# A pad of 384 bytes per partition at the top of SBUF's right side, in a sparse-linear and LoRA-gate kernel

## The chip, the core and the metric

One core of a Trainium2 chip. The metric is the device time of one execution in microseconds (us). Times come from runs on the chip, details from one execution taken by the hardware profiler.

## What is computed

Input is `x`, 2 batches of 1024 rows of 1024 fp32 values. With `xn` the layer norm of each row:

```python
bm  = 32x32 blocks of mask whose sum is > 0
s   = xn @ (W * bm).T + bias                      # 1024 -> 1024
c   = softmax((mean over rows of xn) @ Wq.T @ keys.T / sqrt(128))   # 8 coefficients per batch
g   = silu(xn @ W_org.T + sum_e c[e] * (xn @ down[e]) @ up[e])      # 8 experts of rank 64
out = x + s * g
```

The kernel folds the experts into one matrix for each batch, `Y = W_org.T + down @ (c * up)`, so that each batch needs two products of 1024 x 1024 x 1024: one with the masked `W` ("s") and one with `Y` ("y").

## The kernel before

Every fp32 operand of a large product is split into a high and a low part of type float32r, and each product is three matmuls: high x high, high x low, low x high. Nearly all matmuls have a stationary operand of 128 x 128 and a moving operand of 128 x 512.

**Order of the work.** Batch 0 comes first. A ramp of about 60 us, ordered by hand, normalises rows, masks `W` and runs "s" for the left half of the columns. `phase` (L533), and `s_tile` (L1068) for the last half, then run eight row tiles per half; one row tile is `open_gemm` (L440), 24 matmuls at each of L450, L453 and L454 (stationary `xgrp`, moving `slot`). Between the row tiles stands the folding of `Y`: `y_mul` (L409), 12 matmuls at L414 to L416 (stationary `dhi` or `dlo`, moving `cut`, output `psw`), for batch 0 and then for batch 1. `late_stores` write batch 1's `Y` to DRAM (`yu`, issued at L510), from where it is read back.

Batch 1, from 291.92 us, is done otherwise: `quad` (L1223) computes a unit of the output from seven products of half matrices instead of eight. One product (`product`, L1209) is 12 matmuls, all of L1213: stationary `ow`, moving `xw`. There are eight units (L1074), alternately the first and the second factor of an output piece; each has 84 matmuls, into the PSUM tiles `acc_ps` and `py`. Written out, the order of one unit on TensorE is: product into `acc_ps`, one into `py`, three into `acc_ps`, one into `py`, one into `acc_ps` (unit 0 interleaves its first two; the last unit does its last product in two halves of 256 columns). While a unit runs, ScalarE and VectorE make `ow` for the next one: mask (L1091), sums (L1099), high part (L1105, ScalarE), low part (L1106, VectorE). ScalarE also copies partial sums between PSUM tiles in `quad` (L1243, L1273, and L1220 to SBUF); TensorE's next products wait for these copies. [...]

**Where tiles lie.** A pool is allocated from the left or from the right end of SBUF. L1103 takes `ow[u]` from `opools[u % 2]`: pool `o0` (L1152) is on the right, `o1` (L1300) on the left. So the even units' stationary operand lies on the right, the odd units' on the left, and the moving operand `xw` (L1053) lies on the left for all units. The byte addresses within a partition that the built program has are:

| tiles | side | address | modulo 512 |
|---|---|---|---|
| `slot`, `xgrp`, later `xw` (four) | left | 5728, 38496, 71264, 104032 | 96 |
| `raw`, then `ow` of odd units, `gate` | left | 136800, 151136, from 179808 | 96 |
| `misc`, and `stash`, `mine` | left | 152160, and from 162432 | 96, and 128 |
| `stage`: `ds`, `wo`, `us`, `ws`, `xt`, later `xs`, `rest`, `yt` | right | from 188384 | 480 |
| `dhi`, `dlo`, later `ow` of even units | right | 200672 to 206816, 200672 | 480 |
| `cu`: `cut`, `acc`, `xlate`, `mh`, `ml` | right | 208864 to 229343 | 480 |

PSUM is not touched by the sides.

Of the kernel before, what the change touches and what calls it, by code (L numbers as in the profile page):

```python
# [9 lines left out]
F32 = mybir.dt.float32  # L10
# [7 lines left out]
P = 128  # L18
# [14 lines left out]
def kernel(  # L33
# [28 lines left out]
    def open_pool(name, bufs=1, **kw):  # L62
        cm = tc.tile_pool(name=name, bufs=bufs, reuse_waits="tile", **kw)
        return cm, cm.__enter__()
# [13 lines left out]
    c0pool = for_late("const0", 1)  # L78
    stash_p = for_late("stash", 8)
    stage_l = for_late("stage_l", 2)  # L80
    fold_cms = []
    for_fold = lambda name, bufs: (fold_cms.insert(0, open_pool(name, bufs, side="right")), fold_cms[0][1])[1]
    cupool = for_fold("cu", 5)
# [1283 lines left out]
```

## Time and profile before

| | |
|---|---|
| time, median of 3 runs (lowest, highest) | 451.43 us (451.36, 451.67) |
| the profiled execution's own time | 452.2 us |
| its span, first to last instruction | 450.5 us |
| TensorE clock granted | 0.999 of full |
| weight loads (PEld) busy | 363.7 us, 81% |
| VectorE (DVE), ScalarE (ACT), GpSimd (POOL) busy | 288.9, 175.7, 76.4 us |
| moved by DMA | 90.58 MB, 201 GB/s over the span |

A row of the profile names the line, the engine, the operation and the tiles (out<-in), then the count, the busy time and the mean duration. Two things matter for reading it here. Matmuls are pipelined: the duration of one, from its start to its modelled end, reaches over the start of the next, so that the pace of a row of matmuls is not its mean duration but the distance from one start to the next. And the chain of waits (the work that ended last, followed back from the end) merges neighbouring matmuls of one line and tile to a piece of so many; a piece's length divided by its count is that pace.

### The profile page before, as it was taken

The numbers are of one execution on the slowest core, as the hardware profiler recorded it, in microseconds if no ns is written. First come the engines' busy times: TensorE is split into PE (matmuls) and PEld (weight loads), VectorE is DVE, ScalarE is ACT, GpSimd is POOL, SyncE is SP. The second block draws the span as 40 slices with busy tenths as digits, with TensorE's granted clock in tenths as the row PEclk, the third lists the DMA queues.
The fourth block names the chain that finished last, engine by engine and source line by source line (L and its number), as shares of the span: only waits on it lengthen the run. The fifth ranks groups of instructions, "written<-read, shape, count | busy, mean of one in ns | idle before, by whom it ended". The sixth has DMA issues, their size and how long they took to land.

```text
span 450.5 us, 5791 instructions
## 1 busy us (share of the span) xinstructions
PE 440.4 (98%) x2058; PEld 363.7 (81%) x2058; DVE 288.9 (64%) x478; ACT 175.7 (39%) x291; POOL 76.4 (17%) x93
## 2 busy tenths in 40 slices
PE   8999999999999999999999999999999999999996
PEld 6789888888878888878887788887888888888885
DVE  6989777766627778864466667487456294365625
ACT  4676535454731222233233135067344322441520
POOL 3774210002220313120000000110020030002000
PEclk9999999999999999999999999999999999999999
DMA  8995306677896889896978987865183146218103
GB/s 280 391 353 198 134 25 210 235 240 224 252 291 184 262 259 331 275 346 192 283 211 284 317 244 226 244 178 187 39 187 140 47 112 170 93 23 218 42 1 116
DMA packets 47741, 90.58 MB, mean 201 GB/s; under 512 B 4816, under 2 KB 15328, under 8 KB 47712
## 3 DMA queue, kind: packets, MB, share of 16 engines
q1 hardware_dynamic: 30624, 66.08, 43.7%
q0 software_dynamic: 6624, 16.26, 15.5%
q10 hardware_dynamic: 10464, 7.87, 5.3%
q8 instruction: 16, 0.26, 0.2%
q14 instruction: 13, 0.11, 0.1%
HBM read 70.26 MB, written 19.93 MB: 200 GB/s over the span
## 4 chain that ended last, share of the span: by engine, by line
PE 68%; DVE 11%; DMA 11%; issue 6%; ACT 3%; POOL 1%; SPq 0%; ACTq 0%; DVEq 0%; POOLq 0%
PE acc_ps L1213 25%; PE py L1213 10%; PE acc_ps L454 7%; PE acc_ps L450 7%; PE acc_ps L453 7%; PE psw L416 4%; PE psw L414 4%; PE psw L415 4%; DMA ws<-in_wT_dram 3%; DMA stash<-in_x_dram 2%; DMA yu<-wo 2%; DVE st L145 1%; DVE slot L591 1%; DMA raw<-in_x_dram 1%; DMA raw<-in_mask_dram 1%
## 5 line engine op out<-in xcount | busy, mean ns | idle before, releaser
L1213 PE MATMUL acc_ps<-xw,ow 128*128 128x512 f32 (+1 forms) x492 | 113.3, 387 | 0.0
L1213 PEld LDWEIGHTS acc_ps<-xw,ow 128*128 128x128 f32 x492 | 91.0, 188 | 19.8 <-ACT acc_ps L1273 0.4
L450 PE MATMUL acc_ps<-slot,xgrp 128*128 128x512 f32 (+1 forms) x288 | 106.5, 370 | 0.1
L454 PE MATMUL acc_ps<-slot,xgrp 128*128 128x512 f32 (+1 forms) x288 | 105.7, 367 | 0.7 <-DVE xgrp L603 0.7
L453 PE MATMUL acc_ps<-slot,xgrp 128*128 128x512 f32 (+1 forms) x288 | 105.7, 367 | 0.6 <-DVE slot L591 0.4
L453 PEld LDWEIGHTS acc_ps<-slot,xgrp 128*128 128x128 f32 x288 | 54.4, 189 | 10.7 <-DVE slot L591 2.1
L454 PEld LDWEIGHTS acc_ps<-slot,xgrp 128*128 128x128 f32 x288 | 54.2, 188 | 10.2 <-DVE xgrp L603 1.1
L450 PEld LDWEIGHTS acc_ps<-slot,xgrp 128*128 128x128 f32 x288 | 54.3, 188 | 9.1 <-DVE stash L466 0.3
L416 PE MATMUL psw<-cut,dlo 128*128 128x512 f32 x128 | 50.0, 390 | 1.2 <-DVE dlo L406 1.2
L414 PE MATMUL psw<-cut,dhi 128*128 128x512 f32 x128 | 50.0, 390 | 0.0
L415 PE MATMUL psw<-cut,dhi 128*128 128x512 f32 x128 | 49.8, 389 | 0.0
L1213 PE MATMUL py<-xw,ow 128*128 128x512 f32 x192 | 46.8, 392 | 0.0
L1213 PEld LDWEIGHTS py<-xw,ow 128*128 128x128 f32 x192 | 36.1, 188 | 7.9
L1106 DVE TENSOR_TENSOR ow<-raw,ow 128x1024 fp32r<-128x1024 f32 (+1 forms) x32 | 34.5, 1088 | 10.9 <-ACT ow L1105 10.9
L405 ACT CAST dhi<-ds 128x512 fp32r<-128x512 f32 x32 | 19.7, 617 | 39.3 <-DMA ds<-in_down_dram 17.0
L502 POOL DMA_DIRECT2D stash<-in_x_dram x16 | 14.4, 898 | 121.5 <-DVE stash L499 121.5
L421 DVE TENSOR_TENSOR wo<-wo,psw 128x512 f32<-128x512 f32 x32 | 21.9, 685 | 16.3 <-PE psw L416 16.0
L1105 ACT CAST ow<-raw 128x1024 fp32r<-128x1024 f32 (+1 forms) x32 | 29.4, 941 | 2.2 <-DVE wo L421 1.6
L416 PEld LDWEIGHTS psw<-cut,dlo 128*128 128x128 f32 x128 | 24.0, 188 | 6.6 <-DVE dlo L406 1.6
L414 PEld LDWEIGHTS psw<-cut,dhi 128*128 128x128 f32 x128 | 24.0, 188 | 5.3 <-ACT dhi L405 0.4
L415 PEld LDWEIGHTS psw<-cut,dhi 128*128 128x128 f32 x128 | 24.1, 188 | 5.0
L1196 POOL DMA_DIRECT2D gate<-in_xT_dram x12 | 10.5, 909 | 94.2 <-DVE gate L1190 68.8
(180 smaller groups left out, 480.5 us busy)
## 6 DMA issues: line engine op xcount, KB each, us to landing
ds<-in_down_dram SPq DMA_DIRECT2D x32, 256.0 KB, 3.6
wo<-in_worgT_dram SPq DMA_DIRECT2D x32, 256.0 KB, 3.8
raw<-in_x_dram SPq DMA_DIRECT2D x11, 512.0 KB, 4.8
stash<-in_x_dram POOLq DMA_DIRECT2D x16, 256.0 KB, 5.2
raw<-in_wu_dram SPq DMA_DIRECT2D x8, 512.0 KB, 4.9
yu<-wo ACTq DMA_DIRECT2D x16, 256.0 KB, 4.9
raw<-yu SPq DMA_DIRECT2D x8, 512.0 KB, 3.6
out_dram<-stash ACTq DMA_DIRECT2D x14, 256.0 KB, 3.9
```

The costliest lines, as they stand in the source:

```text
L405: nc.scalar.copy(dhi, ds)
L414: nc.tensor.matmul(ps, lhsT=dhi[:, c, :], rhs=u[c][:, 0, :], start=c == 0, stop=False)
L415: nc.tensor.matmul(ps, lhsT=dhi[:, c, :], rhs=u[c][:, 1, :], start=False, stop=False)
L416: nc.tensor.matmul(ps, lhsT=dlo[:, c, :], rhs=u[c][:, 0, :], start=False, stop=c == 3)
L421: nc.vector.tensor_tensor(ws, ws, ps, ALU.add)
L450: nc.tensor.matmul(ps, lhsT=xs[:, kt, 0, cols], rhs=w[:, kt, 0, wc], start=kt == 0, stop=False)
L453: nc.tensor.matmul(ps, lhsT=xs[:, kt, 0, cols], rhs=w[:, kt, 1, wc], start=False, stop=False)
L454: nc.tensor.matmul(ps, lhsT=xs[:, kt, 1, cols], rhs=w[:, kt, 0, wc], start=False, stop=kt == NKT - 1)
L502: nc.gpsimd.dma_start(res, x[at], accum_op=ALU.add)
L1105: nc.scalar.copy(o[:, a:b, 0], raw[:, a:b])
L1106: nc.vector.tensor_tensor(o[:, a:b, 1], raw[:, a:b], o[:, a:b, 0].bitcast(F32), ALU.subtract)
L1213: nc.tensor.matmul(ps, lhsT=o[:, a, wl, j, :], rhs=xw[j][:, m, xl, cols], start=start and j == 0 and k == 0, stop=j == 3 and k == 2, skip_ ...
```

## The change

Before the first pool of the right side is opened, a pool of one tile of 96 fp32 values per partition is opened there. No instruction reads or writes the tile, and the pool stays open to the end.

```diff
     stage_l = for_late("stage_l", 2)
+
+    align = ctx.enter_context(tc.tile_pool(name="align", bufs=1, side="right"))
+    align.tile([P, 96], F32, name="pad")
     fold_cms = []
     for_fold = lambda name, bufs: (fold_cms.insert(0, open_pool(name, bufs, side="right")), fold_cms[0][1])[1]
     cupool = for_fold("cu", 5)
```

Every tile of the right side moves down by 384 bytes: `ow` of even units from 200672 to 200288, `cut` from 208864 to 208480, `stage` from 188384 to 188000; modulo 512 from 480 to 96. The left side stays where it is. In the two built programs each engine has the same instructions in the same order with the same waits; they differ in the addresses of right-side tiles alone. (The numbers of lines behind the change are 3 higher.)

## The prediction

> **What bounds the kernel now.** I read the page first: engines, then the clock row.
>
> ```profile
> PE 440.4 (98%) x2058; PEld 363.7 (81%) x2058; DVE 288.9 (64%) x478; ACT 175.7 (39%) x291; POOL 76.4 (17%) x93
> ...
> PEclk9999999999999999999999999999999999999999
> ```
>
> TensorE is busy 98% of the span at the full clock. So either it is kept waiting, or its pace counts. The view of waits, for TensorE alone, answers the first:
>
> ```profile
> PE psw L416 <- DVE dlo L406: 1.2, 1, 1.2
> PE warm L672 <- DVE ones_r L93: 1.1, 1, 1.1
> PE sp L357 <- DVE qb L350: 0.9, 1, 0.9
> ```
>
> These are its longest waits, and they end before 292 us. In batch 1 one short wait is left, in unit 0 (below). There the end is set by the pace of the matmuls, so the chain of waits is read next, for units 1 to 3 (pieces: start us, length us, what, count):
>
> ```profile
> 314.55 2.72 PE py L1213 x12
> 317.27 8.16 PE acc_ps L1213 x36
> 325.43 2.72 PE py L1213 x12
> 328.15 5.52 PE acc_ps L1213 x24
> 333.67 2.79 PE py L1213 x12
> 336.46 8.36 PE acc_ps L1213 x36
> 344.82 2.79 PE py L1213 x12
> 347.62 5.49 PE acc_ps L1213 x24
> 353.11 2.72 PE py L1213 x12
> 355.83 8.16 PE acc_ps L1213 x36
> 363.99 2.72 PE py L1213 x12
> ```
>
> The same matmuls have two paces. Unit 1: 8.16 / 36 = 0.2267 us. Unit 2: 8.36 / 36 = 0.2322. Unit 3: 0.2267 again. Mean durations hide it (392 ns for all). Windows cut at the units' first matmuls show that it goes on (window, length, then busy us and count of PE, PEld, DVE, ACT, POOL, clock, DMA share, GB/s):
>
> ```profile
> 330.71:350.23 19.52, 19.52 (x86) 15.83 (x84) 11.53 (x15) 8.22 (x13) 1.83 (x3) 1.00 0.57 146
> 350.23:369.27 19.04, 19.04 (x85) 15.77 (x84) 10.84 (x14) 6.80 (x10) 2.23 (x3) 1.00 0.24 69
> 369.27:388.79 19.52, 19.52 (x86) 15.83 (x84) 10.68 (x14) 6.84 (x10) 1.27 (x2) 1.00 0.59 148
> 388.79:407.83 19.04, 19.04 (x85) 15.77 (x84) 10.84 (x14) 6.80 (x10) 2.25 (x3) 1.00 0.24 70
> ```
>
> Units 2, 4 (and 6) last 19.52 us, units 3, 5 (and 1, 7) 19.04, exactly each time. VectorE and ScalarE do the same work in units 4 and 5 (10.68 and 10.84, 6.84 and 6.80), so their load isn't the cause. What differs by parity is the side of `ow`: in even units the stationary operand begins at 480 modulo 512 and the moving one at 96; in odd units both begin at 96. Is it the place itself or the difference? The folding of `Y` has both operands on the right, both at 480: in the timeline, 27 matmuls of L414 to L416 run from 71.06 to 77.18, 6.12 / 27 = 0.2267. Batch 0's products, both on the left: from 200.26 to 207.97, 34 matmuls, 0.2268. So 480 alone is not slow; the unlike pair is.
>
> **The change, part by part.** No instruction is added or moved; the pad costs none. What can change is the price of instructions with a right-side operand.
>
> *Even units.* After the change `ow` of even units is at 200288. Its distance to `xw` at 5728 is 95 x 2048 bytes, that of the odd units' `ow` (151136) is 71 x 2048: alike modulo 512 and modulo any power of two up to 2048. I take the odd units' pace for the even ones: units 2, 4 and 6 give 3 x (19.52 - 19.04) = 1.44 us. All of it is on TensorE's path: `ow` for unit 3 (L1106) is written up to 347.9 except for pieces used late in unit 3, against a first use at 350.23, and unit 7 is an odd one, so the tail stays.
>
> *Unit 0* is different. Near its end TensorE waits for ScalarE's copy (timeline of ScalarE):
>
> ```profile
> 307.18 1.05 ACT L1105 CAST ow<-raw 128x1024 fp32r<-128x1024 f32 x1 [0.57 <-DMA out_dram<-stash]
> 308.14 0.59 ACT L1273 COPY acc_ps<-acc_ps 128x512 f32<-128x512 f32 x1
> ```
>
> The copy L1273 stands behind L1105, and L1105 waits for a store that frees `stash` (`ow` of unit 1 takes that place). That store hangs on an accumulating DMA issued at 298.88, not on the products. A matmul gains 0.48 / 84 = 5.7 ns. So TensorE, 72 x 5.7 ns = 0.41 us earlier at this point, waits 0.41 longer; only the 12 matmuls behind it gain, 12 x 5.7 ns = 0.07 us. Bounds: 0.07, or, if the store lands earlier, all 84 x 5.7 ns = 0.48 and the wait's 0.23 (unit 0 lasts 19.75 against 19.52) = 0.71. I take 0.07: nothing in the change hastens the store.
>
> *Switches of side.* Where a fold of `Y` (both right) follows or precedes batch 0's products (both left), one matmul at each switch has its successor's weights from the other side. Start to start, these 26 take 5.8 ns more than their neighbours: 26 x 5.8 = 0.15 us. I take 0.15; bounds 0 and 0.15.
>
> *VectorE and ScalarE.* Rows with unlike and like places:
>
> ```profile
> L1063 DVE TENSOR_TENSOR xw<-xs,xw 128x512 fp32r<-128x512 f32 x13 | 8.3, 687 | 7.5 <-ACT xw L1062 7.5
> L1063 DVE TENSOR_TENSOR xw<-misc,xw 128x512 fp32r<-128x512 f32 x12 | 8.1, 685 | 0.8 <-ACT xw L1062 0.8
> ```
>
> `xs` is at 480, `misc` and `xw` at 96: 687 and 685 ns. ScalarE's L1062 takes 620 for both. So 0; even 2 ns on each of VectorE's 478 instructions are 1 us spread beside a TensorE that doesn't wait for them.
>
> *GpSimd.* Its unlike rows (L233 1298 ns for 512 columns, L648 2405 for 1024) are not slower than its like ones (L582 1358, L591 1580). If the unlike became 1580 per 512, the two L648 ahead of its mask work in the ramp would cost 2 x (3160 - 2405) = 1.5 us; VectorE's rows show no such thing, and the forms differ. I take 0, bound +1.5.
>
> *DMA.* The Trainium skill ("DMA: Bandwidth & Descriptors", how a descriptor splits into AXI transactions) says that a read begins at the 256-byte boundary below its start, and bytes before the start still cost beats. A row of 2048 bytes at 480 (224 modulo 256) is 71 beats by that, at 96 it is 67: an estimate of 6% for reads from the right side. `yu<-wo` takes 4.9 us, so at most 0.28 less each. TensorE's wait of 1.2 at L416 hangs partly on such a store, most others are hidden. The trace has no like pair of transfers free of other load; I take 0, bounds -0.3 and +0.3.
>
> *A rule against it all.* The skill's page "SBUF — State Buffer" (who interferes with whom) gives TensorE two independent read ports, one for the moving operand and one for weights, and says that it never waits on anyone. By that rule the places of the two can't matter and the sum is 0: 451.4. By the row it is 19.52 against 19.04. The measured row decides; what inside SBUF makes the difference, the trace doesn't show.
>
> **Sum.** 1.44 + 0.07 + 0.15 = 1.66 us. The profiled execution takes 452.2 (span 450.5 and 1.7 around it) and would take 450.54; the median of runs is 0.77 below it, 451.43 - 1.66 = 449.77. With unit 0's other bound (0.64 more) and the DMA's (0.3 more) it would be 448.83.
>
> **Rivals.**
>
> *No change (451.4).* The slow pace belongs to something else of even units. For it: DMA is busier there (0.59 against 0.24). Against: unit 1 with 0.32 is as fast as unit 5 with 0.24, the products around 200 us keep 0.2268 in slices where DMA is 0.6 to 0.9 busy, and the pace changes at the unit's boundary. Or the pad doesn't do what it says because another modulus counts; the distances above speak against it up to 2048. Chance 0.09.
>
> *Waits take the gain (450.6 to 451.0).* The shorter even units run into copies or `ow` pieces that are late, as in unit 0. For it: in unit 2 VectorE idles 5.8 us for a load of `raw` (L1091), with the sum for `py` (L1257) queued behind it. Against: `py` is ready at 342.4 for a use at 344.66, 2.3 us to spare against 0.4 lost. Half the gain stays: 450.6 or more. Chance 0.06.
>
> *Slower (453.9).* With all of SBUF in one phase, what ScalarE and VectorE write for the next unit meets what TensorE reads, and the 5.7 ns move to matmuls that are free of it now: the odd units' 336 cost 1.9, the folding's 384 cost 2.2, against a gain of 1.66: 451.43 + 4.1 - 1.66 = 453.9. It makes the kernel slower from 1.66 / 0.0057 = 291 such matmuls on. Against: in batch 0 `slot` is written at 96 (L424, L432) while TensorE reads `slot` and `xgrp` at 96, at 0.2268. Chance 0.04.
>
> **Numbers.** The forecast has 0.81; its bounds are 448.83 and, with GpSimd's price half come true (0.75), 450.5. The second rival's near end adds up to 450.6. My range is 448.9 to 450.6, which leaves out no change, slower and most of the second rival. A difference under 0.2% (0.9 us) can't be told from none here. Faster 0.85, same 0.11, slower 0.04.
>
> **What would show it.** In the profile after: even units of 19.04 us, 36-matmul pieces of 8.16 in every unit; unit 0 about 19.7, with a wait before its last product that has grown to some 0.6; VectorE's and ScalarE's rows within 3 ns. Wrong, if even units stay at 19.52 (another cause), if odd ones rise, or if the wait at L416 or the ramp moves by over 0.5 us.

## The result, and the profile after

The median is 449.05 us in 22 runs, against 451.55 in 22 runs of the kernel before: a ratio of 0.9952, 95% interval [0.9939, 0.9965], or 2.2 us less (1.6 to 2.8); the medians differ by 2.5, the means by 2.2. The forecast was 449.77, with a range of 448.9 to 450.6. Single executions of one kernel lie up to 4.3 us apart (447.9 to 452.2 here, 450.1 to 452.7 before), so the gain is seen in many runs or in the profile, not in one time. The profiled execution has a span of 448.7 us against 450.5.

The chain of waits for units 1 to 3 (start us, length us, what, count), to be held against the pieces shown before (L1216 here is L1213 there):

```profile
316.97 8.16 PE acc_ps L1216 x36
325.13 2.72 PE py L1216 x12
327.85 5.44 PE acc_ps L1216 x24
333.29 2.72 PE py L1216 x12
336.01 8.16 PE acc_ps L1216 x36
344.17 2.72 PE py L1216 x12
346.89 5.44 PE acc_ps L1216 x24
```

Every piece of 36 now takes 8.16 us, every piece of 12 takes 2.72: unit 2, from 330.41, runs as fast as unit 1. The windows at the first matmuls of units 0 to 4 (columns as before) say the same:

```profile
292.00:311.37 19.37, 19.34 (x86) 15.69 (x84) 15.59 (x24) 13.71 (x23) 2.02 (x3) 1.00 0.66 188
311.37:330.41 19.04, 19.04 (x86) 15.77 (x84) 10.61 (x14) 8.84 (x14) 1.68 (x2) 1.00 0.35 96
330.41:349.45 19.04, 19.04 (x86) 15.77 (x84) 11.47 (x15) 8.22 (x13) 1.82 (x3) 1.00 0.59 152
349.45:368.49 19.04, 19.04 (x86) 15.77 (x84) 10.89 (x14) 6.80 (x10) 2.23 (x3) 1.00 0.25 69
368.49:387.53 19.04, 19.04 (x86) 15.77 (x84) 10.62 (x14) 6.84 (x10) 1.27 (x2) 1.00 0.59 152
```

Units 2 and 4 lost 0.48 us each. The other engines' busy times and the uneven DMA share (0.59, 0.25) are still those of before, so they were not the cause. Unit 0 has 0.38 us less, and a wait is left in it. The waits of weight loads in batch 1, before and after (us in total, times, longest), and ScalarE's timeline at the same place:

```profile
PEld acc_ps L1213 <- ACT acc_ps L1273: 0.4, 1, 0.4
PEld acc_ps L1216 <- ACT acc_ps L1276: 0.5, 1, 0.5
```

```profile
306.93 1.05 ACT L1108 CAST ow<-raw 128x1024 fp32r<-128x1024 f32 x1 [0.52 <-DMA out_dram<-stash]
307.88 0.58 ACT L1276 COPY acc_ps<-acc_ps 128x512 f32<-128x512 f32 x1
```

The copy still stands behind work that waits for the store. VectorE's rows have not moved:

```profile
L1066 DVE TENSOR_TENSOR xw<-xs,xw 128x512 fp32r<-128x512 f32 x13 | 8.3, 686 | 7.4 <-ACT xw L1065 7.4
L1066 DVE TENSOR_TENSOR xw<-misc,xw 128x512 fp32r<-128x512 f32 x12 | 8.1, 686 | 0.0
```

### The profile page after: what moved, and what is told of

Its sections match the earlier page's. It is cut to its first block, busy times and chain, and to the rows that moved or that the text cites. A ratio compares the mean times of both kernels' runs of the same rounds, so it can differ in the third digit from the quotient of the medians.

```text
span 448.7 us, 5791 instructions
## 1 busy us (share of the span) xinstructions
PE 437.7 (98%) x2058; PEld 363.1 (81%) x2058; DVE 288.9 (64%) x478; ACT 175.3 (39%) x291; POOL 76.5 (17%) x93
## 4 chain that ended last, share of the span: by engine, by line
PE 68%; DVE 12%; DMA 10%; issue 6%; ACT 3%; POOL 1%; SPq 0%; ACTq 0%; DVEq 0%; POOLq 0%
PE acc_ps L1216 24%; PE py L1216 10%; PE acc_ps L457 7%; PE acc_ps L453 7%; PE acc_ps L456 7%; PE psw L419 4%; PE psw L417 4%; PE psw L418 4%; DMA ws<-in_wT_dram 3%; DMA stash<-in_x_dram 2%; DVE st L148 1%; DMA raw<-in_x_dram 1%; DVE slot L594 1%; DMA misc<-in_up_dram 1%; DMA raw<-in_mask_dram 1%
## 5 line engine op out<-in xcount | busy, mean ns | idle before, releaser
L1216 PE MATMUL acc_ps<-xw,ow 128*128 128x512 f32 (+1 forms) x492 | 112.0, 384 | 0.0
L1216 PEld LDWEIGHTS acc_ps<-xw,ow 128*128 128x128 f32 x492 | 90.8, 188 | 18.7 <-ACT acc_ps L1276 0.5
L1216 PE MATMUL py<-xw,ow 128*128 128x512 f32 x192 | 46.3, 389 | 0.0
L1216 PEld LDWEIGHTS py<-xw,ow 128*128 128x128 f32 x192 | 36.0, 188 | 7.5
L409 DVE TENSOR_TENSOR dlo<-ds,dhi 128x512 fp32r<-128x512 f32 x32 | 22.0, 688 | 14.8 <-ACT dhi L408 14.8
L1108 ACT CAST ow<-raw 128x1024 fp32r<-128x1024 f32 (+1 forms) x32 | 29.4, 939 | 2.1 <-DVE wo L424 1.6
```

The source lines that it names most:

```text
L409: nc.vector.tensor_tensor(dlo, ds, dhi.bitcast(F32), ALU.subtract)
L1108: nc.scalar.copy(o[:, a:b, 0], raw[:, a:b])
L1216: nc.tensor.matmul(ps, lhsT=o[:, a, wl, j, :], rhs=xw[j][:, m, xl, cols], start=start and j == 0 and k == 0, stop=j == 3 and k == 2, skip_ ...
```

## The experiments

The theory: TensorE's pace hangs on the distance, modulo 512 bytes, between the places of the weights that it loads and of the operand that it streams. Rivals: a place of 480 is slow by itself; transfers gain from starting at 96; a smaller or larger modulus counts. A unit's length below runs from the start of its first matmul to that of the next unit's first.

**left384: the pad on the other side.**

```diff
+    align = ctx.enter_context(tc.tile_pool(name="align", bufs=1))
+    align.tile([P, 96], F32, name="pad")
     wpool = ctx.enter_context(tc.tile_pool(name="wslot", bufs=2))
```

> The pad of 384 bytes is on the left side instead, ahead of the slots; the right side stays as it was. Both sides then begin at 480 modulo 512. If the pace hangs on the difference between the places of the stationary and the moving operand (my theory), even units take 19.04 us like the odd ones, unit 0 19.1 to 19.75, and the time is that of the right-side pad, a ratio of 0.995 to the kernel before. If a stationary operand at 480 is slow by itself (rival), all eight units take 19.52 and the time is some 1.9 us above the kernel before. If the gain of the right-side pad came from its transfers starting at 96 (rival), the units' pace changes but the rest of the time does not follow: the ratio stays near 1.

Measured: a ratio of 0.9967 [0.9954, 0.9981] to the kernel before. The 0.995 expected lies just outside this interval. Windows of units 2 and 3:

```profile
330.00:349.04 19.04, 19.04 (x86) 15.77 (x84) 11.47 (x15) 8.22 (x13) 1.82 (x3) 1.00 0.60 152
349.04:368.08 19.04, 19.04 (x86) 15.77 (x84) 10.89 (x14) 6.80 (x10) 2.23 (x3) 1.00 0.25 69
```

With both sides at 480 all units but the first take 19.04 us (unit 0: 19.59). So it is the distance that counts, not the place. No right-side transfer starts elsewhere than before (those of the left side do), so the units' gain is not one of right-side transfers that start at 96. Units, switches and unit 0 of this profile give 1.44 + 0.26 + 0.15 = 1.85 us, a ratio of 0.9959 inside the interval. At 0.9 to 2.1 us the interval also leaves room for an effect of transfers of some tenths of a us.

**o0only and foldonly: one part each.** The first opens the pad ahead of the even units' operand, the second with the folding's pools, which are closed before it.

```diff
+        cm_al, al = open_pool("align", 1, side="right")
+        al.tile([P, 96], F32, name="pad")
         cm_o0, opools[0] = open_pool("o0", 1, side="right")
...
```

> The pad of 384 bytes is opened on the right only ahead of the pool of the even units' stationary operand, so batch 0 and the folding keep the right side at 480. My theory: even units 19.04 us as with the full change; the 26 matmuls at switches between folding and batch 0 keep their 5.8 ns (0.15 us in all). Rival (the gain is in batch 0's transfers): even units 19.52.

```diff
+    for_fold("align", 1).tile([P, 96], F32, name="pad")
     cupool = for_fold("cu", 5)
```

> The pad of 384 bytes stands on the right only while batch 0 and the folding run and is closed ahead of the even units' stationary operand, which lies at 480 again. My theory: even units 19.52 us, and the matmuls at switches of side lose their 5.8 ns. Rival: even units 19.04.

Unit 2 of `o0only`, then of `foldonly`:

```profile
329.90:348.94 19.04, 19.04 (x85) 15.77 (x84) 11.47 (x15) 8.23 (x13) 1.82 (x3) 1.00 0.58 152
```

```profile
328.53:348.04 19.51, 19.51 (x85) 15.82 (x84) 11.52 (x15) 8.21 (x13) 1.82 (x3) 1.00 0.56 146
```

The gain in the units comes with the place of `ow`: pools opened behind it move too, but in units 4 and 6 nothing else on the right side is read or written. Each of the two ran once (449.93 and 449.99 us); such single times decide nothing, the units do.

The start times in the traces tell the switches apart as well: the 26 matmuls at switches between folding and batch 0 take 5.9 ns more than 226.7 in `o0only` (5.8 before) and 0.2 ns in `foldonly` (0.5 with the full change). At a switch each matmul has both of its own operands on one side, but while the last one of the old side streams its operand, weights of the other side are loaded. So it is the load for the next matmul that meets the stream of the running one. The interval after it is longer too, by 4 ns in `o0only` and before, and by nothing in the other two: a switch costs 10 ns over two intervals. Why the second is longer is not shown.

**pad128, pad256, pad352, pad192: other sizes.** The same edit as the change with 32, 64, 88 and 48 values instead of 96.

> The pad on the right is 128 bytes: right side at 352 modulo 512, 256 from the left side's 96. If like places modulo 512 are needed (my theory), even units stay slow, 19.2 to 19.8 us. If like places modulo 256 are enough (rival), they take 19.04.

> The pad on the right is 256 bytes: right side at 224 modulo 512, 128 from the left side's 96. Modulo 512 (my theory): even units slow, 19.2 to 19.8 us. If any two places that are 0 to 256 apart were good and only those beyond it bad (rival), 19.04.

> The pad on the right is 352 bytes: right side at 128 modulo 512, only 32 from the left side's 96. If only equal places run at the fast pace (my theory in its strict form), even units are above 19.1 us; if the cost grows with the distance (rival), they take 19.04 to 19.1.

> The pad on the right is 192 bytes: right side at 288 modulo 512, 192 from the left side's 96 (and -64 modulo 256). After the pads of 128 and 352 bytes my theory is now that the two operands must be a multiple of 256 bytes apart: even units then stay slow, 19.5 to 19.6 us. If a multiple of 64 that isn't 128 is good too (rival), 19.04.

Unit 2 of each, in this order:

```profile
329.12:348.17 19.05, 19.05 (x86) 15.78 (x85) 11.48 (x15) 8.22 (x13) 1.82 (x3) 1.00 0.60 152
```

```profile
330.61:350.12 19.51, 19.51 (x85) 15.82 (x84) 11.52 (x15) 8.21 (x13) 1.81 (x3) 1.00 0.55 148
```

```profile
330.54:350.13 19.59, 19.59 (x86) 15.80 (x84) 11.55 (x15) 8.20 (x13) 1.81 (x3) 1.00 0.58 148
```

```profile
330.68:349.90 19.22, 19.22 (x85) 15.79 (x84) 11.49 (x15) 8.21 (x13) 1.81 (x3) 1.00 0.57 151
```

Here the theory fell in one point. Two operands 256 bytes apart modulo 512 (pad of 128) run as fast as equal ones, as the rival in the expectation had it: the modulus is 256. The other sizes fit 256 too: the kernel before, 384 apart, and the pad of 256, 128 apart, are both 128 modulo 256 and have one pace. Right side minus left, modulo 256, against the mean pace of even units 2, 4 and 6 in the start times:

| kernel | distance, bytes | modulo 256 | ns per matmul |
|---|---|---|---|
| change, left384 | 0 | 0 | 226.7 |
| pad128 | 256 | 0 | 226.7 |
| before, pad256, foldonly | 384, 128, 384 | 128 | 232.3 |
| pad192 | 192 | 192 | 228.9 |
| pad352 | 32 | 32 | 233.3 |

The rival that the cost grows with the distance fell as well: 32 bytes apart is the slowest. The pad of 192 is slow, but at 19.22 us less so than the 19.5 to 19.6 expected: the theory says which distance is free, not what the others cost. Distances of 32 and 192 were tried in one placement each. Single times of the four, 449.16, 452.07, 452.26 and 451.26 us in the order above, are no evidence by themselves.

**o0_896: the larger moduli.**

```diff
-        cm_xs, xs_pool = open_pool("xs", 4, side="right")
+        cm_al, al = open_pool("align", 1, side="right")
+        al.tile([P, 224], F32, name="pad")
...
+        cm_xs, xs_pool = open_pool("xs", 3, side="right")
...
-                res = pools_b1["tmp"].tile([P, NH], F32, name="rest", tag="rest", bufs=3)
+                res = pools_b1["tmp"].tile([P, NH], F32, name="rest", tag="rest", bufs=2)
...
```

> As the pad ahead of the even units' stationary operand alone, but with 896 bytes (384 + 512): like the moving operand modulo 512, 512 bytes apart modulo 1024. To make room, the staging tiles of unit 0 are 3 instead of 4 and those of the last unit 2 instead of 3, so unit 0 and unit 7 may wait. If 512 is the modulus (my theory), units 2, 4 and 6 take 19.04 us; if it is 1024 or 2048 (rival), 19.2 to 19.6.

Units 2, 4 and 6 took 19.04 us, with their operand 512 bytes off modulo 1024. With fewer staging tiles unit 0 took 22.47 us, and the kernel ended 8.7 us after the start of its last matmul instead of 4.0. That makes the time (456.18 in one run) useless; the units answer the question.

**copyfirst: the wait in unit 0.** On top of the change (`slot(3)` is a function of `quad` here: it runs the jobs that write the first pieces of the next unit's `ow`):

```diff
             after(3)
-            slot(3)
             product(u, 2, 5, pb, False)
+            if u > 0:
+                slot(3)
...
                 nc.scalar.copy(pa, pb)
+            if u == 0:
+                slot(3)
```

> The full change, and in unit 0 the jobs that write the first pieces of the next unit's stationary operand are moved behind the copy that TensorE waits for (L1273). If that copy waits on ScalarE only because it stands behind the work that waits for a store (my theory of unit 0), TensorE's wait before unit 0's last product is gone and unit 0 takes 19.04 to 19.1 us (19.37 with the change alone); later units stay at 19.04; the time is about 0.3 us below the change's. If unit 1's operand comes late for it (rival), unit 1 takes more than 19.04 and the 0.3 us are given back.

Measured: 0.996 [0.9941, 0.998]. ScalarE's timeline, and the windows of units 0 and 1:

```profile
303.80 0.58 ACT L1274 COPY acc_ps<-acc_ps 128x512 f32<-128x512 f32 x1
304.32 2.00 ACT L1105 CAST ow<-raw 128x1024 fp32r<-128x1024 f32 x2
```

```profile
289.31:308.35 19.04, 19.04 (x85) 15.77 (x84) 15.09 (x24) 13.15 (x22) 2.02 (x3) 1.00 0.65 188
308.35:327.39 19.04, 19.04 (x85) 15.77 (x84) 11.11 (x14) 9.30 (x14) 1.67 (x2) 1.00 0.33 100
```

The copy goes ahead, unit 0 takes 19.04 us, and unit 1 doesn't wait. The wait came from the order of work on ScalarE, as the theory of unit 0 says. That the time is 0.3 us below the change's is not shown.

**pad384_again, pad128_timed, copyfirst_again: three versions on one chip.** No new edit.

> The change itself, on the same chip as the next two. Gain by the units' lengths and the switches of side 1.4 + 0.15 us and what of unit 0 isn't waited away (0.1 to 0.4): ratio to the kernel before 0.996 to 0.9965.

> The pad of 128 bytes, timed. If a multiple of 256 bytes between the two operands is all that counts (my theory now), its ratio is that of the pad of 384 bytes within 0.15%, and even units take 19.04 us again. If the rest of the full pad's gain comes from like places modulo 512 (rival), it stays 0.15% or more behind.

> The pad of 384 bytes with the copy ahead in unit 0, beside the pad alone on one chip: unit 0 19.04 us, the wait of 0.3 to 0.5 us gone, the ratio 0.0007 to 0.001 below the pad's, which is under what these rounds can tell; the unit's length in the profile decides.

| kernel | median us | ratio to before, 95% interval | unit 0 us |
|---|---|---|---|
| pad384_again | 448.54 | 0.9945 [0.9928, 0.9963] | 19.49 |
| pad128_timed | 448.65 | 0.995 [0.9927, 0.9972] | 19.39 |
| copyfirst_again | 448.87 | 0.9952 [0.9936, 0.9968] | 19.04 |

The pad of 128 is as good as that of 384 within these intervals, as modulus 256 asks; even units took 19.04 us again. The first ratio lies below the 0.996 to 0.9965 expected, of which its interval takes in the lower end only; the expectation had the switches at 0.15 us, which is too little (see below). Unit 0 without its wait is shorter in both profiles of `copyfirst`, but the time doesn't show it: 0.3 us drown in waits that change from run to run. That version isn't shown to be faster than the change.

## Why the prediction was right

- **The pace of even units** was nearly the whole case, and its term held: 1.44 us forecast for units 2, 4 and 6, 3 x 0.48 = 1.44 by the windows.
- **Which distance counts** was put right as far as it went (alike modulo every power of two up to 2048 is enough), but too strictly in the theory taken to the chip: 256 is enough. The no-change rival's doubt about the modulus was right in so far as it isn't 512; that cost nothing here, since a multiple of 2048 is one of 256.
- **The switches of side** were sized too low. The prediction counted one interval of each, 26 x 5.8 ns = 0.15 us, and overlooked the next one. Over both intervals the 26 switches cost 0.26 us before and 0.01 after: a gain of 0.25.
- **Unit 0** was sized too low as well, though its mechanism held. TensorE's wait was to grow by the 0.41 us that it arrived earlier. In the start times of this pair the two drawn-out matmuls exceed the pace by 0.22 us before and 0.31 after, because L1108 started 14.93 us after the unit's first matmul instead of L1105's 15.26: the store had landed earlier. Gain 0.38 instead of 0.07. It scatters: the fast pace gave unit 0 between 19.37 and 19.59 us in six profiles, the pace of 232.3 between 19.52 and 19.75 in three, in two of which (`foldonly`, `pad256`) the wait cost 0.05 us at most. Means 19.43 and 19.61, a gain of 0.18. That the change hastens the store is not shown.
- **The sum**: 1.44 + 0.25 + 0.18 to 0.38 is 1.9 to 2.1, against 1.66 forecast and 2.2 (1.6 to 2.8) measured. The rest is within the interval.
- **"Mean durations hide it (392 ns for all)"** was a misreading. The row's mean mixes even and odd units; by the trace, unit 2 has a mean of 394.5 ns and unit 3 of 389.1. After the change the same row, shown here below that of before, has 389:

```profile
L1213 PE MATMUL acc_ps<-xw,ow 128*128 128x512 f32 x468 | 110.3, 392 | 0.0
L1216 PE MATMUL acc_ps<-xw,ow 128*128 128x512 f32 x468 | 109.0, 389 | 0.0
```

- **VectorE and GpSimd, at 0**: 686 for 687 and 685 ns; GpSimd's L651 (L648 before) takes 2403 for 2405. The bound of 1.5 us is gone.
- **DMA, at 0**: `yu<-wo` lands in 5.2 us (median) instead of 4.9, so the fewer beats estimated from the Trainium skill ("DMA: Bandwidth & Descriptors", how a descriptor splits into AXI transactions) are not seen. `left384`, where right-side transfers start as before, keeps the units' gain. An effect under the scatter of landing times stays open.
- **The rule of two ports that never wait** (the Trainium skill's "SBUF — State Buffer", who interferes with whom) was taken to make the sum 0. The runs contradict that for these matmuls: the same loads and streams cost 226.7 to 233.3 ns by the distance of their places.
- **Slower**: odd units stayed at 19.04 us and the folding at its pace with everything in one phase, so writes of ScalarE and VectorE brought no new collision.
- **One sign of being wrong came true**: in the profile after, the ramp is 0.6 us later. The change is not the reason as far as the runs show. `o0only`, which leaves the ramp's tiles where they were, is 0.5 us later too, and a second profile of one and the same kernel differs by as much (`pad128` 0.5 later, `pad128_timed` 0.1 earlier).

In the profiled pair the span fell by 1.7 us only. Units 0, 2, 4 and 6 gave 1.8 us; ahead of 291.9 us the gains at switches and at the wait for `dlo` were used up by the later ramp and by longer waits at the mask's and the coefficients' small matmuls (`mp` L274 1.2 for 0.5, `sp` L360 1.4 for 0.9). Batch 1 began between 288.4 and 292.0 us in the 14 profiles, and 0.4 to 0.9 us apart in two of one kernel, so nothing is put down to the change there.

## What to carry to other kernels

Where TensorE is always busy, read its pace from start to start, stretch by stretch: two paces of the same matmul, with the same clock and no waits, are a cost that busy shares hide and that a row's mean duration blurs, since it mixes the stretches. Then ask what differs between the stretches; the bytes at which the tiles lie belong to that list, and tiles from two ends of memory get their offset by accident. Here a pad of 128 bytes would have done; what counts is the distance between weights and moving operand, so either side can be moved.

## What was not expected of the hardware

The pace of 128x512 float32r matmuls depends on the distance between the streamed operand and the weights loaded meanwhile, with a period of 256 bytes as far as these runs go: 226.7 ns at 0, 228.9 at 192, 232.3 at 128, 233.3 at 32. The cost doesn't simply grow with the distance, and it is regular: in unit 2 the distances between starts repeat, 241, 232, 231, 232, 228, 230, 233 ns, whatever the other engines do. What inside SBUF or TensorE makes it is not settled; other operand types and sizes weren't tried.
